# A graph network's messages: shares of target and features computed in input order and scattered as 2 KB rows, instead of small rows scattered and targets' rows gathered

## The chip, the cores and the metric

The kernel runs on one core of a Trainium2 chip. A core has TensorE (matrix products into PSUM), VectorE, ScalarE, GpSimd and SyncE, which run side by side and wait for each other through semaphores, and 16 DMA engines that move data between HBM and SBUF. DMAs are issued by SyncE and ScalarE (for transfers whose addresses are known to the issuing engine) and by GpSimd (for indirect ones, whose row numbers lie in SBUF). The metric is the device time of the whole program in microseconds, the median of several runs.

## The reference

3125 nodes have 256 features each; 50000 edges have a source, a target and 16 features. The edges come sorted by target; the sources are random, and the targets are dense at low numbers (3125 u², with u uniform). The computation, with `LN` a layer norm without weights:

```python
h = relu(LN(x))
msg = relu(concat(h[src], h[dst], edge_attr) @ mW1 + mb1)      # 50000 x 512
agg = segment_sum(msg @ mW2 + mb2, src)                        # by source
x = x + h + (relu(concat(h, agg) @ uW1 + ub1) @ uW2 + ub2)
g = relu(LN(x))
for W, b in three_layers:                                      # gelu between the layers
    g = D^-1/2 (A + I)^T D^-1/2 (g @ W) + b                    # A counts edges, D the in-degrees
out = x + g
```

The kernel splits `mW1` by rows: the source's share of a message is `h @ W1a`, the target's `h @ W1b`, the features' `edge_attr @ W1c`. The first two are tables with a row for each node (table A and table B). The sum by source comes ahead of `mW2`, which is linear.

## The kernel before, in words

**Names.** A node tile is 125 nodes; there are 25 of them (t). Node n belongs to tile n % 25. An edge tile is 128 edges of one source tile. "Products in two pieces" means that a fp32 value is split into a rounded part and a remainder (type fp32r), each multiplied in a pass of its own; plain fp32 products take two records each in the trace.

**Sort (L185 to L511).** The edges have to be grouped by source tile. They are dealt into 391 columns of 128; the first 240 columns are part 0, the last 151 part 1. For chunks of 24 columns `sort_chunk` (L330) makes each edge's place: keys are read back as broadcasts (L219), compared with the partition number (L336), counted by a running sum on VectorE (L345, L348), and turned by small products (L354). Each edge's payload is 20 numbers, 80 bytes: 16 features, target, source in its tile, column (L386 to L389). GpSimd scatters a column of 128 payloads by an indirect DMA (L170): part 0's columns in the sort, part 1's between the gathers of the next stage (L808). The places are first filled with an empty payload (L240, on ScalarE's queue). Two lists of work are laid between the chunks (L503 to L511): `tables` (L416: turns h, two fp32 products of 512 columns for each node tile at L427, and stores of table A, 4 KB a row in two pieces, L432, and table B, 2 KB a row, L437) and the counting of in-degrees (L456 to L486: one-hots on ScalarE at L470 and L473, comparisons on VectorE at L462).

**Messages (L588 to L826).** A flag in SBUF says whether the data keep the limits that the tiling assumes; it is read into a register and a branch chooses this path (L1067 to L1075). `order` (L776) runs over part 0, 25 targets' tiles of KT[0] = 11 edge tiles each, then part 1 with 7 each: 450 edge tiles. `load` (L620) fetches a tile's sorted payloads and 125 rows of table A. For each edge tile, `edge_tile` (L722) does:

```python
gather gb <- tabB[target]                       # GpSimd, L725, 128 rows of 2 KB
p  = payT @ wE                                  # features, L730
p += ohT @ apc                                  # source's share by a one-hot, two pieces, L732
gb += p                                         # VectorE, L733
m[0] = relu(gb); m[1] = max(gb, 0) - m[0]       # ScalarE L735, VectorE L736
p_sum += oh^T @ m                               # sum by source, two pieces, L746
```

One edge tile's sums are issued after the next one's `edge_tile`. Beside it goes `adjacency` of the step before (L704): counts of edges between nodes, as products of one-hots of sources and of targets (L681 on VectorE, 626 columns; L683 on TensorE, twice 313), for five ranges of targets, with 20 products of ranges in part 0 and 16 in part 1 for each tile. `counted` (L694) copies them to A as bytes; part 1 adds to what part 0 left (L701). Part 0's sums wait in HBM (`R_d`, L753) until part 1 fetches them (L759). In part 1, `node_steps` (L527) runs the node update of tile t - 2 beside (lines L539 to L574, TensorE tile `nd`).

**Graph layers and output (L951 to L1021).** 25 products with W (L974), then for 7 stretches of 448 columns 25 x 4 products with A (L1004), whose bytes VectorE and ScalarE turn into fp32r by turns (L998, L1000); three layers; then 25 transposed tiles are added to x and stored (L1021).

Of the kernel before, what the change touches and what calls it, by code (L numbers as in the profile page):

```python
# [19 lines left out]

# [10 lines left out]
BF16 = mybir.dt.bfloat16  # L31
# [10 lines left out]
NT, NP = 25, 125  # L42
EP, EC = 125, 400
SC = E // P
LEFT = E - P * SC
SCOLS = SC + 1
SPLIT = 240
CH = 24
CHUNKS = [(c, min(CH, e - c)) for b, e in ((0, SPLIT), (SPLIT, SCOLS)) for c in range(b, e, CH)]
PARTS = 2  # L50
KT = (11, 7)
NG, GT = 5, 5
GW = GT * NP
GS = GW + 1
HALF = GS // 2

REACH = (((0, 2), (1, 4), (3, 6), (5, 8), (6, 10)), ((0, 1), (0, 3), (1, 4), (3, 5), (4, 6)))
NB = NT * NG
AW = 448
NA = (NG * GS + AW - 1) // AW  # L60
NPAD = NA * AW
PW = 20
C_DST, C_PS, C_COL = ED, ED + 1, ED + 2
EPS = 1e-5
assert NT * NP == N and EP * EC == E and NB <= P and GS % 2 == 0


def col(c):

    return c // GT * GS + c % GT * NP  # L70
# [3 lines left out]
def gnn(ctx: ExitStack, tc: tile.TileContext, x, src, dst, ea, mW1, mb1, mW2, mb2, uW1, ub1, uW2,  # L74
# [3 lines left out]
    ORDER = mybir.DependencyInfo(mybir.DependencyClass.NoSync, mybir.DependencyReason.DATA)  # L78
# [5 lines left out]
    bk_d = dram.tile([SCOLS, P], BF16, name="bk_d")  # L84

    n_rows = [NT * k * P for k in KT]
    rows_d = [dram.tile([n + P * SCOLS, PW], F32, name=f"rows_d{q}") for q, n in enumerate(n_rows)]
    rows_v = [
        rows_d[q][:n_rows[q], :].rearrange("(t p k) w -> t p (k w)", p=P, k=KT[q])
        for q in range(PARTS)  # L90
    ]
    tabA = dram.tile([NT * NP, 2 * H], F32, name="tabA")
    tabB = dram.tile([N, H], F32, name="tabB")
    hT_d = dram.tile([NT, P, 2, NP], F32, name="hT_d")
    R_d = dram.tile([NT, NP, H], F32, name="R_d")
    xs_d = dram.tile([N, D], F32, name="xs_d")
    dis_d = dram.tile([NT, NP], F32, name="dis_d")
    xsv = xs_d.rearrange("(p c) f -> p c f", c=NT)
# [5 lines left out]
    key_s = g1.tile([P, SCOLS], I32, name="key_s")  # L104
    key_d = g1.tile([P, SCOLS], I32, name="key_d")
    for key, v in ((key_s, src), (key_d, dst)):
        nc.vector.memset(key[:, SC:], 0)
        nc.sync.dma_start(key[:, :SC], v[:P * SC].rearrange("(p c) -> p c", c=SC))
        nc.sync.dma_start(key[:LEFT, SC:], v[P * SC:].rearrange("(p o) -> p o", o=1))
# [4 lines left out]
    iota_i = g1.tile([P, P], I32, name="iota_i")  # L114
    nc.gpsimd.iota(iota_i, pattern=[[1, P]], base=0, channel_multiplier=0)
    iota_f = const.tile([P, P], F32, name="iota_f")
    nc.vector.tensor_copy(iota_f, iota_i)
    pid_i = g1.tile([P, 1], I32, name="pid_i")
# [4 lines left out]
    nc.vector.memset(ones, 1.0)  # L123

# [7 lines left out]
    dis = const.tile([NP, NT], F32, name="dis")  # L132
    flag = const.tile([1, 1], I32, name="flag")
    late = SCOLS - SPLIT
    pay1 = hold.tile([P, late, PW], F32, name="pay1")
    place1 = hold.tile([P, late], I32, name="place1")
# [12 lines left out]
    def ln_stats(pool, mv, row):  # L149
        st = pool.tile([NP, 6], F32, name="ln_st", bufs=3)  # L150
        nc.vector.bn_stats(st, row)
        nc.vector.bn_aggr(mv, st)

    def ln_scale(pool, mv):

        ve = pool.tile([NP, NT], F32, name="ln_ve")
        rstd = pool.tile([NP, NT], F32, name="ln_rstd")
        nmr = pool.tile([NP, NT], F32, name="ln_nmr")
        nc.vector.tensor_scalar(ve, mv[:, :, 1], EPS, None, op0=ALU.add)
        rsqrt(pool, rstd, ve, NP, NT)  # L160
        nc.vector.scalar_tensor_tensor(nmr, mv[:, :, 0], -1.0, rstd, op0=ALU.mult, op1=ALU.mult)
        return rstd, nmr


    fills = [[], []]
    scatters = [[], []]

    def scatter(q, place, pay, behind=None):

        s = nc.gpsimd.indirect_dma_start(  # L170
            out=rows_d[q], in_=pay, in_offset=None,
            out_offset=bass.IndirectOffsetOnAxis(ap=place, axis=0))
        tc.declare_no_dep(s.ins, group=f"rows{q}", reason="every edge has a place of its own")
        tc.add_to_no_dep_group(f"rows{q}", s.ins)
        for f in fills[q]:
            tc.add_manual_dep(s.ins, f.ins.name, SYNC, reason="places are filled first")
        if behind is not None:
            tc.add_manual_dep(s.ins, behind.ins.name, ORDER, reason="in turn with the gathers")
        scatters[q].append(s)

    def sorted_rows(q, load):
        for s in scatters[q]:
            tc.add_manual_dep(load.ins, s.ins.name, SYNC, reason="all rows are in place")

    with s1:  # L185
        gps = s1.enter_context(tc.tile_pool(name="gps", bufs=1, space=PSUM))
        ones_p = gps.tile([P, 1], F32, name="ones_p")
        nc.vector.memset(ones_p, 1.0)

        def parts_of(key, name):  # L190

            p_i = g1.tile([P, SCOLS], I32, name=f"p_{name}")
            c_f = g1.tile([P, SCOLS], F32, name=f"c_{name}")
            nc.vector.tensor_scalar(p_i, key, 5243.0, None, op0=ALU.mult)
            nc.vector.tensor_single_scalar(p_i, p_i, 17, op=ALU.logical_shift_right)
            nc.vector.scalar_tensor_tensor(c_f, p_i, -float(NT), key, op0=ALU.mult, op1=ALU.add)
            nc.vector.scalar_tensor_tensor(c_f[:, SC:], none, -64.0, c_f[:, SC:], op0=ALU.mult,
                                           op1=ALU.add)
            return p_i, c_f

        none = g1.tile([P, 1], F32, name="none")
        nc.vector.tensor_scalar(none, pid, LEFT - 0.5, None, op0=ALU.is_ge)
        psi, cs = parts_of(key_s, "s")
        pdi, cd = parts_of(key_d, "d")
        g_i = g1.tile([P, SCOLS], I32, name="g_i")
        nc.vector.tensor_scalar(g_i, cd, 13.0, None, op0=ALU.mult)
        nc.vector.tensor_single_scalar(g_i, g_i, 6, op=ALU.arith_shift_right)
        bkey = g1.tile([P, SCOLS], F32, name="bkey")
        nc.vector.scalar_tensor_tensor(bkey, cs, float(NG), g_i, op0=ALU.mult, op1=ALU.add)
        BT = P  # L210
        n_t = (SCOLS + BT - 1) // BT
        p_bk = gps.tile([P, n_t * P], F32, name="p_tab", bufs=2).rearrange("p (t a) -> p t a", a=P)
        bkT = g1.tile([P, n_t, P], BF16, name="bkT")
        bk = {}

        def load_keys(j):
            c0, w = CHUNKS[j]
            bk[j] = g1.tile([P, P * CH], BF16, name="bk", bufs=2)
            nc.sync.dma_start(  # L219
                bk[j][:, :P * w],  # L220
                bk_d[c0:c0 + w, :].rearrange("(o c) p -> o (c p)", o=1).to_broadcast([P, P * w]))

        for i in range(n_t):
            n = min(BT, SCOLS - i * BT)
            nc.tensor.transpose(p_bk[:n, i, :], bkey[:, i * BT:i * BT + n], ident)
        for i in range(n_t):
            n = min(BT, SCOLS - i * BT)
            nc.vector.tensor_copy(bkT[:n, i, :], p_bk[:n, i, :])
            nc.sync.dma_start(bk_d[i * BT:i * BT + n, :], bkT[:n, i, :])
            if i < 2:  # L230
                load_keys(i)


        fill = g1.tile([P, max(KT), PW], F32, name="fill")
        nc.gpsimd.memset(fill, 0.0)
        nc.gpsimd.memset(fill[:, :, C_PS:C_COL + 1], -1.0)
        for q in range(PARTS):
            for t in range(0, NT, GT):
                w = KT[q] * PW
                fills[q].append(nc.scalar.dma_start(  # L240
                    rows_v[q][t:t + GT].rearrange("t p w -> p t w"),
                    fill[:, :KT[q], :].rearrange("p k w -> p (k w)").unsqueeze(1)
                    .to_broadcast([P, GT, w])))


        cs_b = g1.tile([P, SCOLS], BF16, name="cs_b")
        nc.vector.tensor_copy(cs_b, cs)
        g_b = g1.tile([P, SCOLS], BF16, name="g_b")
        nc.vector.tensor_copy(g_b, g_i)
        eq_g = g1.tile([P, NG, SCOLS], BF16, name="eq_g")  # L250
        for b in range(NG):
            nc.vector.tensor_scalar(eq_g[:, b, :], g_b, float(b), None, op0=ALU.is_equal)
        eq_s = g1.tile([P, NT, SCOLS], BF16, name="eq_c", bufs=1)
        for b in range(NT):
            nc.vector.tensor_scalar(eq_s[:, b, :], cs_b, float(b), None, op0=ALU.is_equal)
        cnt = g1.tile([NT, PARTS, NG], F32, name="cnt")
# [73 lines left out]
        def sort_chunk(j):  # L330
# [6 lines left out]
            if j + 2 < len(CHUNKS):  # L337
                load_keys(j + 2)
# [100 lines left out]
        for c in range(NT):  # L439
            work.append(lambda c=c: tables(c))  # L440
# [661 lines left out]
```

## Time and profile before

| what | value |
|---|---|
| median of 3 runs | 2251.86 us (2247.84 to 2256.53) |
| the profiled execution | 2433.28 us, its span 2431.6 us |
| mean granted TensorE clock | 0.916 |
| TensorE busy | 1948.0 us, 80% of the span |
| VectorE busy | 1561.4 us, 64% |
| ScalarE busy | 1010.5 us, 42% |
| GpSimd busy | 858.9 us, 35% |
| moved by DMA | 242.64 MB, 100 GB/s over the span |
| chain that ended last | TensorE 58%, VectorE 12%, DMA 7%, ScalarE 5% |

The profiled execution is one run under the hardware profiler, and is longer than the runs that make the median; all rows of the profile belong to it. In a row of a group, `x450 | 454.6, 1010` means 450 instructions, 454.6 us busy in all, 1010 ns for one; what follows is the idle time of the engine just before them and what ended most of it. `PEld` is the loading of weights, which runs beside PE's products. In the list of queues the columns are packets, MB, and the time that the packets took as a share of the time of 16 DMA engines. "Issue" stands for time in which an engine waited for nothing that the profile shows.

### The profile page before, as it was taken

What the parts mean: (1) busy time and instruction counts of PE and PEld (TensorE: products, weight loads), DVE (VectorE), ACT (ScalarE), POOL (GpSimd) and SP (SyncE); (2) the same over time, 40 slices, a digit from 0 to 9 for tenths busy, and PEclk for the clock granted to TensorE, in tenths of its full rate; (3) what the DMA queues carried; (4) which work ended last, traced back from release to release, by engine and by line L of the source; (5) the groups of instructions that cost most, each with busy time, mean ns of one, the idle gap of its engine ahead of it and who ended that gap; (6) DMA issues with size and microseconds to landing.
All of it is one profiled execution on the core that took longest, in us unless ns stands there. A gap on an engine that the chain in (4) does not pass through costs nothing.

```text
span 2431.6 us, 30795 instructions
## 1 busy us (share of the span) xinstructions
PE 1948.0 (80%) x10314; PEld 1570.6 (65%) x10314; DVE 1561.4 (64%) x3618; ACT 1010.5 (42%) x2070; POOL 858.9 (35%) x895
## 2 busy tenths in 40 slices
PE   3224554675888888888889999999996999999993
PEld 3223232354665666665667888888885898998992
DVE  4636343595877888887879999999983323223221
ACT  0415443452444545454444444444433544434440
POOL 0656656304666666666653332333210000000000
PEclk9999666776999899999989999999997999999995
DMA  7102343325544444444444444444432000000003
GB/s 223 43 6 82 101 148 86 101 102 160 152 135 135 130 140 140 136 140 131 136 135 143 142 142 136 144 141 142 142 86 77 22 1 1 1 1 1 1 1 107
DMA packets 117792, 242.64 MB, mean 100 GB/s; under 512 B 19790, under 2 KB 65348, under 8 KB 117491
## 3 DMA queue, kind: packets, MB, share of 16 engines
q0 software_dynamic: 48512, 122.02, 18.5%
q1 hardware_dynamic: 55996, 103.64, 13.2%
q10 hardware_dynamic: 13108, 14.84, 2.0%
q8 instruction: 85, 1.39, 0.2%
q14 instruction: 91, 0.75, 0.1%
HBM read 193.31 MB, written 47.12 MB: 99 GB/s over the span
## 4 chain that ended last, share of the span: by engine, by line
PE 58%; DVE 12%; issue 7%; another core or an unknown queue 7%; DMA 7%; ACT 5%; POOL 2%; ACTq 1%; SPq 0%; DVEq 0%; POOLq 0%
PE p_o L1004 17%; PE p_A L683 8%; PE p_sum L746 7%; PE p_x L732 7%; PE nd L563 4%; PE p_x L730 3%; DVE gb L733 3%; PE p_g L974 2%; DVE od L681 2%; DVE m L736 2%; PE p_tab L427 2%; PE tr L665 2%; DMA out<-xrow 2%; PE nd L572 2%
## 5 line engine op out<-in xcount | busy, mean ns | idle before, releaser
L725 POOL DMA_INDIRECT gb<-tabB,rows x450 | 454.6, 1010 | 590.0 <-DVE m L736 410.2
L170 POOL DMA_INDIRECT rows_d<-pay,place x391 | 398.1, 1018 | 254.1 <-issue 116.6
L1004 PE MATMUL p_o<-a,g 125*128 125x448 f32 x2100 | 443.1, 370 | 0.0
L1004 PEld LDWEIGHTS p_o<-a,g 125*128 125x128 f32 x2100 | 394.7, 188 | 32.4 <-ACT g L976 0.3
L746 PE MATMUL p_sum<-m,oh 128*125 128x512 f32 x900 | 389.5, 466 | 18.8 <-issue 8.2
L735 ACT ACTIVATE m<-gb 128x512 fp32r<-128x512 f32 x450 | 283.4, 634 | 227.8 <-DVE gb L733 161.3
L683 PE MATMUL p_A<-od,oh_h 128*125 128x313 f16 x1800 | 360.5, 305 | 21.3 <-ACT A L697 11.1
L733 DVE TENSOR_TENSOR gb<-gb,p_x 128x512 f32<-128x512 f32 x450 | 305.0, 678 | 81.3 <-remote 24.7
L732 PE MATMUL p_x<-apc,ohT 125*128 125x512 f32 x900 | 344.5, 430 | 8.9 <-ACT ohT L667 6.7
L736 DVE SCALAR_TENSOR_TENSOR m<-gb,m 128x512 fp32r<-128x512 f32 x450 | 306.4, 684 | 64.7 <-ACT m L735 43.4
L681 DVE TENSOR_SCALAR od<-iota_h,dloc 128x626 f16<-128x626 f16 x900 | 331.6, 397 | 7.9 <-PE p_A L683 6.4
L683 PEld LDWEIGHTS <-oh_h 128*125 128x125 f16 x1800 | 246.8, 140 | 95.4 <-issue 35.0
L998 DVE CAST a<-A 125x448 fp32r<-125x448 uint8 x262 | 102.8, 393 | 273.7 <-PE p_o L1004 273.5
L1000 ACT CAST a<-A 125x448 fp32r<-125x448 uint8 x263 | 148.7, 566 | 240.8 <-PE p_o L1004 240.8
L730 PE MATMUL p_x<-wE,payT 128*128 128x512 f32 x450 | 209.7, 466 | 25.4 <-DVE gb L733 20.7
L746 PEld LDWEIGHTS p_sum<-m,oh 128*125 128x125 f32 x900 | 172.7, 196 | 80.5 <-ACT m L735 17.6
L732 PEld LDWEIGHTS p_x<-apc,ohT 125*128 125x128 f32 x900 | 174.7, 198 | 32.8 <-ACT ohT L667 13.3
L427 PE MATMUL p_tab<-wAB,hT 128*125 128x512 f32 x200 | 126.7, 791 | 73.6 <-issue 46.2
L354 PE MATMUL p_pos<-ones_r,q 128*128 128x2 f32 x391 | 83.0, 323 | 72.4 <-DVE carry L351 40.4
L427 PEld LDWEIGHTS p_tab<-wAB,hT 128*125 128x125 f32 x200 | 48.6, 256 | 134.5 <-issue 104.7
L354 PEld LDWEIGHTS p_pos<-ones_r,q 128*128 128x128 f32 x391 | 72.8, 262 | 86.8 <-issue 42.4
L668 ACT CAST oh_h<-oh 128x375 f16<-128x375 f32 (+1 forms) x125 | 71.2, 569 | 135.8 <-DVE oh L659 121.6
(193 smaller groups left out, 2437.9 us busy)
## 6 DMA issues: line engine op xcount, KB each, us to landing
apc<-tabA SPq DMA_DIRECT2D x50, 500.0 KB
tabA<-a_sb SPq DMA_DIRECT2D x25, 500.0 KB
bk<-bk_d SPq DMA_DIRECT2D x16, 768.0 KB
gb<-tabB,rows POOLq DMA_INDIRECT x450
rows_d<-pay,place POOLq DMA_INDIRECT x391
tabB<-b_sb SPq DMA_DIRECT2D x25, 250.0 KB
R_d<-R SPq DMA_DIRECT2D x25, 250.0 KB
R<-R_d SPq DMA_DIRECT2D x25, 250.0 KB
```

Of the source, the lines that this page charges most:

```text
L170: s = nc.gpsimd.indirect_dma_start(out=rows_d[q], in_=pay, in_offset=None, out_offset=bass.IndirectOffsetOnAxis(ap=place, axis=0))
L427: nc.tensor.matmul(p, hT[:, k, :], wAB[:, s, k, :], start=k == 0, stop=k == 1)
L681: nc.vector.tensor_scalar(od, iota_h, dloc[q, t][:, g, k:k + 1], None, op0=ALU.is_equal)
L683: nc.tensor.matmul(p[:, h_, :HALF], oh_h[q, t][:, k, :], od[:, h_ * HALF:(h_ + 1) * HALF], start=k == lo, stop=k == hi)
L725: gathers[0] = nc.gpsimd.indirect_dma_start(out=gb, out_offset=None, in_=tabB, in_offset=bass.IndirectOffsetOnAxis(ap=row[q, t][:, k, C_DS ...
L730: nc.tensor.matmul(p, payT[q, t][:, k // 2, :], wE[k % 2], start=True, stop=False)
L732: nc.tensor.matmul(p, ohT, apc[q, t][:, s, :], start=False, stop=s == 1)
L733: nc.vector.tensor_add(gb, gb, p)
L735: nc.scalar.activation(m[:, 0, :], gb, AF.Relu)
L736: nc.vector.scalar_tensor_tensor(m[:, 1, :], gb, 0.0, m[:, 0, :].bitcast(F32), op0=ALU.max, op1=ALU.subtract)
L746: nc.tensor.matmul(p_sum[t], oh, m[:, s, :], start=k == 0 and s == 0, stop=k == KT[q] - 1 and s == 1)
L1004: nc.tensor.matmul(po[:, f, :AW], g[:, s, q, f * P:(f + 1) * P], a, start=s == 0 and q == 0, stop=s == NT - 1 and q == 1)
```

## The change

Node n now belongs to tile n // 125 (L240, a product and a shift). The 391 columns of edges become 66 blocks of 768 consecutive edges, which, being sorted by target, have targets in a stretch of 128 nodes. The places come from products with a triangular matrix for all edges at once (L269 to L291). The stage has three pieces.

*The lead (to L443).* Keys and x are loaded; ScalarE issues a fill of zeros, 20.3 MB in runs of 6.3 KB, after x has landed (L216); LN, relu and transposes of h; GpSimd adds h and ub2 to x for the residual (L402, L403, 50 additions of 256 columns); table B in two pieces, 4 KB a row (26 products of 512 columns, each of two fp32 halves; 13 stores of 1 MB).

*The blocks of z (L446 to L593).* For each block a register is loaded with the first target of its stretch, and 128 rows of table B are loaded from there; features are split in two pieces and transposed; targets' one-hots come from a broadcast product. TensorE forms the features' plus the target's share, 512 numbers for each edge, ScalarE and VectorE copy them from PSUM, and GpSimd scatters them with the source's and target's number as rows of 2112 bytes, 391 scatters in all. Beside this go table A's products and stores (13 of 1 MB, on ScalarE's queue) and the counting of sources.

*Messages.* One pass over 25 tiles of 17 edge tiles: 425. Rows are loaded in groups of 4, 4, 3, 3 and 3 edge tiles into three buffers. The one-hots of targets are 14131 columns wide for each tile t in all. The in-degrees are read from A when all counts are there (L829 to L856). The node update runs for t - 1, with one buffer for each of its tiles.

```diff
-KT = (11, 7)
+BLK = MB * P
+KT = 17
+ZW = 528
...
+        fill = nc.scalar.dma_start(
+            rows_d[:ROWS, :].rearrange("(t s) w -> t s w", s=CAP)[:, SURE:, :]
+            .rearrange("t (p i) w -> p t (i w)", p=P),
+            zero.unsqueeze(1).to_broadcast([P, NT, (KT - SURE // P) * ZW]))
+        for v in x_in:
+            tc.add_manual_dep(fill.ins, v.ins.name, SYNC, reason="x is wanted first")
...
+        def window(b):
+            bw[b] = z1.tile([P, 2 * H], F32R, name="bw", bufs=4)
+            eng = nc.scalar if b % 3 == 2 else nc.sync
+            reg = eng.value_load(w0_i[0:1, b:b + 1], min_val=0, max_val=N - P)
+            eng.dma_start(bw[b].bitcast(F32), tabB[bass.ds(reg, P), :])
...
+        def block(b):
+            z = zt[b % 3]
+            cols = range(MB) if b < NB - 1 else (MB - 1,)
+            nc.vector.tensor_copy(z[:, :, H:H + 2], ends[:, :, b, :])
+            for j0 in range(0, MB, 2):
...
+                p = gps.tile([P, 2, H], F32, name="p_z", bufs=2)
+                for j in js:
+                    o = p[:, j - j0, :]
+                    nc.tensor.matmul(o, pay[b][:, j // 2, :], wE[j % 2], start=True, stop=False)
+                    for s in range(2):
+                        nc.tensor.matmul(o, one[b][:, j, :], bw[b][:, s * H:(s + 1) * H],
+                                         start=False, stop=s == 1)
+                a, e = js[0], js[-1] + 1
+                (nc.vector.tensor_copy if j0 == 2 else nc.scalar.copy)(
+                    z[:, a:e, :H], p[:, a - j0:e - j0, :])
+                for j in js:
+                    s = nc.gpsimd.indirect_dma_start(
+                        out=rows_d, in_=z[:, j, :], in_offset=None,
+                        out_offset=bass.IndirectOffsetOnAxis(ap=place[:, j, b:b + 1], axis=0))
...
+        def store_A(c):
+            def f(b, e, n, v):
+                nc.scalar.dma_start(tabAv[c + b:c + e, :NP, :].rearrange("t p f -> p t f"), v)
+            return f
...
+        def load_rows(t, i):
+            a, e = GROUPS[i]
+            v = mp.tile([P, 4, ZW], F32, name="z", bufs=3)[:, :e - a, :]
+            o = nc.sync.dma_start(
+                v, rows_d[t * CAP + a * P:t * CAP + e * P, :].rearrange("(k p) w -> p k w", p=P))
+            for s in scatters:
+                tc.add_manual_dep(o.ins, s.ins.name, SYNC, reason="all rows are in place")
...
-        def edge_tile(q, t, k):
-            oh, ohT = onehot[q, t, k]
-            gb = mp.tile([P, H], F32, name="gb", bufs=5)
-            gathers[0] = nc.gpsimd.indirect_dma_start(
-                out=gb, out_offset=None, in_=tabB,
-                in_offset=bass.IndirectOffsetOnAxis(
-                    ap=row[q, t][:, k, C_DST:C_DST + 1].bitcast(I32), axis=0))
+        def edge_tile(t, k):
+            oh, ohT, zr = onehot[t, k]
             p = mps.tile([P, H], F32, name="p_x", bufs=2)
-            nc.tensor.matmul(p, payT[q, t][:, k // 2, :], wE[k % 2], start=True, stop=False)
             for s in range(2):
-                nc.tensor.matmul(p, ohT, apc[q, t][:, s, :], start=False, stop=s == 1)
-            nc.vector.tensor_add(gb, gb, p)
+                nc.tensor.matmul(p, ohT, apc[t][:, s, :], start=s == 0, stop=s == 1)
+            gb = mp.tile([P, H], F32, name="gb", bufs=3)
+            nc.vector.tensor_add(gb, zr, p)
```

## The prediction

> **What bounds the kernel now.** I read the split by stage first, because the busy shares of the page mix stages with different limits. The stage borders come from the trace: the flag that opens the messages is read at about 557 us, part 0 ends at 1294, the messages at 1847, and the first large graph product starts at 1905.
>
> ```profile
> core 0: us, PE busy (x) PEld busy (x) DVE busy (x) ACT busy (x) POOL busy (x), PEclk, DMA share, GB/s
> 0.00:60.00 60.00, 23.87 (x407) 22.83 (x407) 25.58 (x108) 4.39 (x16) 3.48 (x44) 1.00 0.73 222
> 60.00:557.00 497.00, 234.17 (x1025) 154.26 (x1025) 268.01 (x567) 205.17 (x547) 241.52 (x250) 0.80 0.29 84
> 557.00:1294.00 737.00, 620.51 (x2890) 452.41 (x2891) 583.15 (x1253) 354.03 (x640) 458.55 (x437) 0.91 0.49 141
> 1294.00:1847.00 553.00, 544.99 (x3494) 477.13 (x3493) 510.52 (x1301) 220.54 (x436) 155.31 (x164) 0.99 0.44 129
> ...
> 1905.00:2375.00 470.00, 468.86 (x2291) 426.33 (x2289) 147.42 (x333) 193.34 (x352) 0.00 (x0) 1.00 0.01 1
> ```
>
> In the sort (60 to 557) no engine is busy for more than 54% of the time; it is a chain that changes engine. Part 1 (553 us) and the graph layers (470 us) are TensorE's, with VectorE at 92% in part 1. Part 0 (737 us) has TensorE at 84% and GpSimd at 62%. The granted clock in the messages is 0.91 and 0.99, so the clock is not the limit there.
>
> The chain of waits shows TensorE's own period in part 1: the same step of the node update ends on the chain every 21.82 us.
>
> ```profile
> 1.71 30.07 DMA xt<-in_x
> ...
> 1354.28 1.78 PE nd L563 x16
> ...
> 1376.10 1.78 PE nd L563 x16
> ```
>
> From such rows come prices back to back: 1.78/16 = 0.111 us for a fp32 pass of 125 columns, 0.203 us for 448 columns (117.57 us for 580 products of the graph layers), so 0.232 for 512 and 0.142 for 313. One target of part 1 is then 7 tiles x 5 x 0.232 = 8.1, 11 transposes = 1.2, 32 count products x 0.142 = 4.5, node update 7.95 (48 passes of 0.111, 8 of 0.216, ten-odd short ones): 21.8 us. The model gives the period exactly, and I use it for the changed loop.
>
> The costly groups give what GpSimd pays for an indirect transfer, and the list of queues what such bytes cost:
>
> ```profile
> L725 POOL DMA_INDIRECT gb<-tabB,rows x450 | 454.6, 1010 | 590.0 <-DVE m L736 410.2
> L170 POOL DMA_INDIRECT rows_d<-pay,place x391 | 398.1, 1018 | 254.1 <-issue 116.6
> ```
>
> ```profile
> q0 software_dynamic: 48512, 122.02, 18.5%
> ```
>
> A scatter takes 1.02 us of GpSimd, with 0.30 us after it in which it waits for nothing visible. Queue q0 held 0.185 x 16 x 2431.6 = 7197 engine-us for 122 MB, nearly all gathered rows: 59 ns per KB on an engine. Scatters of 80-byte rows alone are seen from 150 to 200 us, in the list of queues of that stretch:
>
> ```profile
> q0 software_dynamic: 768, 0.25, 3.1%
> ```
>
> That is 0.031 x 16 x 50 = 24.8 engine-us for 0.25 MB, 99 ns per KB, in packets of some 325 bytes.
>
> **The new message loop.** Gathers (450), their rows, the payload products of 512 columns (450), the transposes of payloads, R's way through HBM, the second pass over A (L701) and the second part's waste (450 tiles become 425) leave. There remain, for each of 25 targets' tiles, 17 edge tiles with two p_x and two sum products each: 68 x 0.232 = 15.8 us; 17 transposes 1.9; counts over ranges of 14131 columns in all (part 0 and 1 had 36 x 626 = 22536) x 0.203/448 = 6.4; node update 7.95. TensorE: 32.0 us. VectorE by part 1's durations: gb 17 x 0.68 = 11.5, m 11.6, one-hots 3.0, small ones 1.5, targets 14131/626 x 0.39 = 8.9, node 1.3: 37.8. Part 1's durations sum to 24.8 for each target against 20.4 us busy (510.5/25), a factor 0.825 for overlapping ends: 31.2 us. Two engines stand within 3% of each other, so I take 34 us a period (bounds 32.5, TensorE alone with part 1's fill of 98.5%, and 37, where they take turns). ScalarE has 17 x 0.63 + 7 copies, some 20 us, and hides. Row loads are 4.6 MB in a period, 135 GB/s, what part 0 already carried at 0.49 of the queues; three buffers of four tiles cover them. Sum: 14 us of hand-over and first rows, 24 for the first target, 24 x 34 = 816, 40 at the end (31 before, and 10 for the in-degrees that now come last): 894, where the two parts took 737 + 553 = 1290. Gain 396 us.
>
> **The lead to the first scatter.** ScalarE issues x's loads, then the 20 MB fill. Before, issuing 6400 small runs kept it until 53.9 us; now 3200 runs of 6.3 KB follow x's landing at about 32 us: free at 41 if issue alone counts, at 125 if the whole fill must land (20.3 MB at 222 GB/s); I take 55, as the queue takes part of them. Ranks by products cost TensorE and VectorE little, beside x. Then 66 register loads of window starts, 22 on ScalarE ahead of its own relus: the only row near is the hand-over, where flag, register, branch and first DMA take 4 us (88 us for 22); the page "DMA: Bandwidth & Descriptors" of the Trainium skill (Latency and other measured facts) has a floor of about 0.6 us (13 us). I take 25. Fifty GpSimd additions of 256 columns (0.3 to 0.7 us, the lower from VectorE's 0.68 for 512) trail by up to 35 us, 26 products of table B and their stores 57 us (L427: 1.27 us a product). First scatter: about 170 us (bounds 125 to 230).
>
> **The z blocks.** 66 blocks, each with six scatters of 128 rows of 2112 B. GpSimd: 391 x (1.02 + 0.30) = 516 us. Queues, for one block: six scatters of 264 KB x 59 ns/KB / 16 = 5.98 us, a window of 512 KB 1.6 us, features 0.15: 7.75, x 66 = 512 us. TensorE has 5.4 us a block, ScalarE and VectorE about 4 each. Two equal limits of 512 us that rarely coincide, so some is added. No row shows scatters of 2 KB rows: by size they are like the gathers (59 ns/KB), by direction like the small scatters (99). I take 59, because 2 KB rows were the gathers' size too and small packets cost more for each byte; 99 is the upper bound, and a rival. Two rules bear on the sum.
>
> First, VectorE beside descriptor writing. The timeline of the sort has
>
> ```profile
> 134.14 0.96 POOL L170 DMA_INDIRECT rows_d<-pay,place  x1 [0.30 <-issue]
> 135.25 0.27 DVE L462 TENSOR_SCALAR eq_c<-cs_b 128x391 bf16<-128x391 bf16 x1 [1.13 <-issue]
> 135.40 0.96 POOL L170 DMA_INDIRECT rows_d<-pay,place  x1 [0.30 <-issue]
> 136.65 0.32 DVE L462 TENSOR_SCALAR eq_c<-cs_b 128x391 bf16<-128x391 bf16 x1 [1.14 <-issue]
> ```
>
> VectorE, with 0.27 us of work in each and nothing to wait for, gets one through for each scatter, 1.26 us apart. The Trainium skill's "SBUF — State Buffer", Who interferes with whom, says why: both engines share a port pair under an exclusive lock, and an operation in a two-port mode waits for the whole of the other's. VectorE's 3 or 4 such operations of a block would wait 1.1 us each: 4 + 4.3 = 8.3 us, 548 us in all. Had the operations other forms, 4 us a block would hide and z would stay at 512.
>
> Second, table A's stores (13 of 1 MB, in the first 20 blocks). x's load above is 3.2 MB on 125 partitions and took 30.07 us: 106 GB/s while all queues moved 222. The skill's "DMA: Bandwidth & Descriptors" (Why a DMA increments its semaphore by 16 and not by 1) gives a transfer the largest number of engines up to 16 that divides its slowest dimension: 125 partitions get 5. By it 12.8 MB at 49.5 ns/KB (queue q1) are 127 us on each of five engines instead of 40 on all: those engines, which also carry scatters, end up to 85 us late. Without the rule z would be 512; with both I take 595 (bounds 430, where GpSimd's 0.30 vanishes and the queues run ahead, and 660).
>
> **Sum.** 170 + 595 + 894 + 585 for the graph layers and output, which keep their sizes, = 2244 us of span against 2431.6. The profiled execution took 2433.28 us, 181 more than the median of 2251.86, and the trace doesn't say where. Spread evenly, the new median is 2251.86 x 2244/2431.6 = 2078. If all of it lies in sort and part 0 (1294 us, which then are 1113 outside the profile), the lead and z shrink by the same 0.86 and the others not: 658 + 894 + 585 = 2137. I take 2105.
>
> **Rivals.**
> - *Likeliest* (0.50): as summed, 2040 to 2160.
> - *Cheap scatters* (0.18): GpSimd issues every 1.0 us and the stores hide; z is about 440, 155 us less, some 1965 (1930 to 2040). For it: 1.018 is the mean in the sort, and part of the 0.30 may be the wait for places. Against: 381 of its 391 waits are named issue.
> - *TensorE and VectorE alternate in the loop* (0.19): 37 us a period, +75: 2180 (2160 to 2240). For it: part 0, with both at 79 to 84%, never filled either. Against: part 1.
> - *Slower than before* (0.10): writing rows to HBM costs more than reading them. From the median, 147 us more in z eat the gain: z of 742; without the 83 us that I added for stores and ports, 659, or 10.0 us a block; less 1.75 for window and features, 8.2 us for 48 rows on each engine: 172 ns a row, 83 ns/KB. Above that it is slower; with the small scatters' 99 ns/KB a block takes 6 x 264 x 99/16 = 9.8, + 1.75 = 11.55 us, z 11.55 x 66 + 83 = 845, and the time is 2105 + 250 x 0.93 (2105/2244, to the median's scale) = 2340 (2263 to 2400). For it: the small scatters themselves. Against: their packets are a sixth of these rows.
> - *No change* (0.03): two of the bad ends together, 2240 to 2263.
>
> A measurement of this kernel can tell about 0.5% from no change, 11 us. Faster 0.87, same 0.03, slower 0.10. The range leaves out the slow case, no change and the low end of cheap scatters: 1975 to 2220.
>
> **What would show it.** In the changed profile: scatters about 1.3 us apart and z near 9 us a block; GpSimd's idle time named as its own issue, not a DMA; on five queues more time than on the others in the first 20 blocks; the node update's step every 34 us with TensorE and VectorE both over 90%; first scatter near 170 us; graph layers at 470. I am wrong if scatters wait for earlier scatters through z's buffers (rows dearer than the 122 ns of 59 ns/KB), or if loop periods pass 37.

## The result: no change, and the profile after

The changed kernel takes 2257.95 us (median of 16 runs) beside 2256.35 us of the kernel before (16 runs): a ratio of 1.0006, interval 0.9993 to 1.002. The forecast was 2105, with a range of 1975 to 2220. Its profiled execution has a span of 2256.6 us, 12.6 us from the 2244 that the prediction summed. So the sum for the new kernel held to 0.6%, and the baseline that it was scaled by did not. The table of stretches of the changed kernel (span, then busy time of each engine, granted clock, share of the DMA engines, GB/s):

```profile
core 0: us, PE busy (x) PEld busy (x) DVE busy (x) ACT busy (x) POOL busy (x), PEclk, DMA share, GB/s
0.00:60.00 60.00, 9.62 (x59) 6.81 (x59) 32.84 (x127) 7.70 (x14) 10.72 (x38) 1.00 0.95 356
60.00:180.00 120.00, 84.77 (x253) 40.69 (x253) 84.46 (x165) 30.95 (x47) 32.34 (x49) 0.80 0.59 221
180.00:800.00 620.00, 455.35 (x1947) 329.53 (x1945) 258.75 (x458) 168.93 (x208) 384.65 (x391) 0.85 0.71 247
...
860.00:1652.00 792.00, 790.85 (x4479) 626.66 (x4478) 741.86 (x1648) 493.34 (x965) 0.00 (x0) 1.00 0.50 161
...
1731.00:2199.00 468.00, 467.90 (x2287) 425.55 (x2286) 145.75 (x330) 192.98 (x351) 0.00 (x0) 1.00 0.00 1
```

The lead ends at 180, the z blocks run to about 800, the message loop has TensorE busy for 99.9% of its time, and the graph layers take 468 us, as before. Below stand two of the costliest groups of the changed kernel, its scatters and the addition that took the old gathers' rows, and then five of its waits in the z blocks (total, times, longest):

```profile
L537 POOL DMA_INDIRECT rows_d<-zt,place x391 | 384.7, 984 | 250.0 <-ACT zt L534 101.8
L758 DVE TENSOR_TENSOR gb<-z,p_x 128x512 f32<-128x512 f32 x425 | 289.5, 682 | 22.6 <-PE p_x L756 19.6
```

```profile
DVE zt L521 <- DMA rows_d<-zt,place: 228.7, 58, 13.1
POOL rows_d L537 <- ACT zt L534: 101.8, 29, 25.4
POOL rows_d L537 <- issue: 91.4, 300, 0.3
...
ACT a_sb L417 <- DMA tabA<-a_sb: 52.1, 8, 10.1
...
DVE zt L534 <- issue: 0.4, 2, 0.2
```

GpSimd pays 0.98 us for a scatter in the mean and 0.3 us behind it, near the 1.02 and 0.30 of the forecast; ScalarE waits for table A's stores eight times. VectorE stands 228.7 us for z's buffers, whose rows are still being scattered.

### The profile page after: what moved, and what is told of

It is laid out like the page before. It is cut to its first block, busy times and chain, and to the rows that moved or that the text cites. A ratio compares the mean times of both kernels' runs of the same rounds, so it can differ in the third digit from the quotient of the medians.

```text
span 2256.6 us, 27379 instructions
## 1 busy us (share of the span) xinstructions
PE 1922.6 (85%) x9541; PEld 1509.0 (67%) x9541; DVE 1341.7 (59%) x2903; ACT 961.9 (43%) x1728; POOL 427.7 (19%) x477
## 5 line engine op out<-in xcount | busy, mean ns | idle before, releaser
L537 POOL DMA_INDIRECT rows_d<-zt,place x391 | 384.7, 984 | 250.0 <-ACT zt L534 101.8
L756 PE MATMUL p_x<-apc,ohT 126*128 126x512 f32 x850 | 325.0, 452 | 1.0 <-ACT ohT L712 0.9
L758 DVE TENSOR_TENSOR gb<-z,p_x 128x512 f32<-128x512 f32 x425 | 289.5, 682 | 22.6 <-PE p_x L756 19.6
L531 PE MATMUL p_z<-bw,ohd 128*128 128x512 f32 x782 | 287.6, 453 | 0.0
L534 ACT COPY zt<-p_z 128x1024 f32<-128x1024 f32 x131 | 132.3, 1010 | 300.6 <-PE p_z L531 288.1
L529 PE MATMUL p_z<-wE,payT 128*128 128x512 f32 x391 | 185.0, 473 | 75.7 <-DVE zt L534 51.4
L729 PE MATMUL p_A<-od,oh_h 128*126 128x448 f16 (+2 forms) x1000 | 230.0, 315 | 0.3 <-DVE od L722 0.3
L531 PEld LDWEIGHTS p_z<-bw,ohd 128*128 128x128 f32 x782 | 171.2, 221 | 52.1 <-issue 19.6
L722 DVE TENSOR_SCALAR od<-iota_h,dloc 128x896 f16<-128x896 f16 (+16 forms) x425 | 176.3, 433 | 0.5 <-PE p_A L729 0.2
L756 PEld LDWEIGHTS p_x<-apc,ohT 126*128 126x128 f32 x850 | 150.9, 191 | 22.0 <-ACT ohT L712 2.2
L521 DVE COPY zt<-ends 128x12 f32<-128x12 f32 x66 | 13.1, 198 | 228.8 <-DMA rows_d<-zt,place 228.7
```

Of the source, the lines that this page charges most:

```text
L529: nc.tensor.matmul(o, pay[b][:, j // 2, :], wE[j % 2], start=True, stop=False)
L531: nc.tensor.matmul(o, one[b][:, j, :], bw[b][:, s * H:(s + 1) * H], start=False, stop=s == 1)
L537: s = nc.gpsimd.indirect_dma_start(out=rows_d, in_=z[:, j, :], in_offset=None, out_offset=bass.IndirectOffsetOnAxis(ap=place[:, j, b:b + 1 ...
L722: nc.vector.tensor_scalar(targets[k][:, :WIDTH[k]], iota_h[:, :WIDTH[k]], dloc[t][:, k:k + 1], None, op0=ALU.is_equal)
L729: nc.tensor.matmul(p_A[g][:, l - g * AW:h - g * AW], oh_h[t][:, k, :], targets[k][:, l - FIRST[k]:h - FIRST[k]], start=start, stop=stop)
L756: nc.tensor.matmul(p, ohT, apc[t][:, s, :], start=s == 0, stop=s == 1)
```

## The experiments

Runs were taken in sets: the kernels of one set ran side by side with the kernel before, and each ratio below is to the kernel before in the same set.

**First: which baseline?** Theory: the 175 us by which the first profile exceeded the runs of the kernel before belong to that execution. Rival: profiling slows the kernel before. Three more kernels cut it (and the changed one) into stages.

e1, the kernel before unchanged. 

> The kernel before, unchanged, profiled a second time. Theory (the 175 us by which its first profiled execution exceeded its runs belong to that one execution, not to the kernel): a new span of 2250 to 2265 us, like the runs, and by stage sort + part 0 shorter by about 175 us. Rival (profiling itself slows something that the kernel before has and the changed one has not): a span of about 2430 again beside runs of 2256.

e2, the kernel before up to the end of the sort (the loop over the two branches is replaced):

```diff
-    for f, fast, general in ((flag, messages, messages_by_column), (flag2, gcn, gcn_by_column)):
...
+    nc.sync.dma_start(out, xs_d)
```

> The kernel before up to the end of the sort; messages and graph layers are left out and the residual is copied to the output. In the first profile the sort took 557 us. If the 175 us lie in the sort: about 385 + 25 for the copy. If they lie in part 0 of the messages: about 557 + 25. If evenly spread: about 515 + 25.

e3, the same copy behind the messages. 

> The kernel before without the graph layers; the output is a copy of the node features after the messages. In the first profile this point was at 1847 us. If all of the 175 us lie ahead of it: about 1672 + 25. If evenly spread: 1710 + 25. Less the time of the sort alone it gives the messages' own time.

e4, the changed kernel up to the end of the z blocks, with the same copy. 

> The changed kernel up to the end of the z blocks; messages and graph layers are left out and the residual is copied to the output. Its profile has this point at about 810 us. Whatever the theory, 810 + 25; against the sort alone it gives what the new stage costs more: about 425 us if the sort really takes 385, 250 if it takes 557.

Measured: e1 2267.44 us (ratio 1.0005, 0.9965 to 1.0046), its profile's span 2265.4. e2 489.58, e3 1699.34, e4 816.8. e1's profiled execution lies among its other runs (2260.7 to 2271.2), so the profiler is not the cause; the first profile showed a longer execution. e3 fits the case of all the excess ahead of the layers (1672 + 25); e2 fits none of its three (410, 582 and 540). Stretches of e1:

```profile
core 0: us, PE busy (x) PEld busy (x) DVE busy (x) ACT busy (x) POOL busy (x), PEclk, DMA share, GB/s
...
60.00:490.00 430.00, 225.51 (x1025) 150.32 (x1025) 264.40 (x565) 203.23 (x547) 243.95 (x250) 0.82 0.33 97
490.00:1130.00 640.00, 588.50 (x2906) 428.43 (x2907) 584.91 (x1259) 354.03 (x644) 464.85 (x438) 0.98 0.56 163
1130.00:1679.00 549.00, 541.56 (x3473) 474.09 (x3472) 507.33 (x1293) 218.25 (x432) 154.40 (x163) 0.99 0.44 129
```

The sort takes 490 us instead of 557 and part 0 640 instead of 737; part 1 and the layers are the same. By two marks: the first p_x product comes at 507.4 instead of 574.0 (67 us earlier), and from there to the first graph product (p_g) it is 1188.0 instead of 1287.6 (100 less). Together 166 us, the whole difference of the spans. The shares of the chain that ended last hint at what it was. The kernel before, first profile (the table at the top of this document lists four of these):

```profile
PE 58%; DVE 12%; issue 7%; another core or an unknown queue 7%; DMA 7%; ACT 5%; POOL 2%; ACTq 1%; SPq 0%; DVEq 0%; POOLq 0%
```

and of e1:

```profile
PE 50%; DVE 17%; DMA 17%; POOL 8%; issue 7%; ACT 2%; DVEq 0%; SPq 0%; ACTq 0%; POOLq 0%
```

"Another core or an unknown queue" was 7.4% of 2431.6 us, 180 us, on a kernel that runs on one core. In e1 the entry is gone. Its size is that of the excess, but its parts are not: of the pieces that the chain lists, 110 us are in the sort and 68 in part 0, where the marks give 67 and 100. In part 0 TensorE was also busy for longer, 620.5 us against 588.5, at a granted clock of 0.91 against 0.98 (the stretches in the prediction and above). What such a wait looks like, in the first profile's timeline, where it is named "remote":

```profile
787.78 0.96 POOL L725 DMA_INDIRECT gb<-tabB,rows  x1 [0.30 <-issue]
...
790.50 0.69 DVE L733 TENSOR_TENSOR gb<-gb,p_x 128x512 f32<-128x512 f32 x1 [3.38 <-remote]
790.59 0.58 ACT L653 CAST payT<-tr 128x512 fp32r<-128x512 f32 x1 [6.75 <-remote]
```

ScalarE stands although what it needs is recorded as made (TensorE's transposes ended by 786.8), and VectorE and ScalarE go on within 0.1 us of each other.

**Second: why do the z blocks take 620 us, not 512?** Theory: ScalarE, in order, waits for the store of table A's last piece with the blocks' copies behind it. Rivals: the five engines of a 125-partition store (the prediction's second rule); VectorE and GpSimd holding each other up (its first); the queues as a whole.

e5 lays table A's 13 pieces evenly over the 66 blocks:

```diff
-        while tests:
-            work.append(tests.pop(0))
+        n_a, n_t = len(work), len(tests)
+        for i in range(n_a, 0, -1):
+            while len(tests) > n_t * (i - 1) // n_a:
+                work.insert(i, tests.pop())
```

> The changed kernel with table A's 13 pieces laid evenly over the 66 blocks instead of one after the other at their start. Theory (the z stage has a slow first half because each piece's copy on ScalarE waits for the store of the piece ahead of it, 25 us on five engines, with the blocks' own copies queued behind; after that GpSimd sets 6 x 1.26 = 7.6 us a block): z from 640 to about 520 us, the kernel about 120 us faster, 2140. Rival (queues are the limit, the same bytes remain): z stays at about 620, within 1% of 2257.

e6 issues each store as two:

```diff
-                nc.scalar.dma_start(tabAv[c + b:c + e, :NP, :].rearrange("t p f -> p t f"), v)
+                for p0, p1 in ((0, 112), (112, NP)):
+                    nc.scalar.dma_start(
+                        tabAv[c + b:c + e, p0:p1, :].rearrange("t p f -> p t f"), v[p0:p1])
```

> The changed kernel with each of table A's stores issued as two, of 112 and of 13 partitions. If stores are slow because 125 partitions are spread over five engines, 112 partitions take 16 of them and a store lands in some 10 us instead of 25: waits for it vanish and z falls by 60 to 110 us, 2150 to 2200. If they are slow because all queues are full of scatters: no change, 2257.

e7 has both. 

> Both edits. If each of them alone removes the wait, together no more than the better one: about 2140. If GpSimd's 1.26 us for each of 391 scatters are the floor, z cannot be under 493 us, so the kernel not under about 2115.

e8 has e5's edit, and the middle copy on ScalarE:

```diff
-                (nc.vector.tensor_copy if j0 == 2 else nc.scalar.copy)(
+                nc.scalar.copy(
```

> The even spread, and the middle copy out of PSUM on ScalarE too, so that VectorE has one long operation less in each block. If VectorE and GpSimd hold each other up in z (the exclusive port pair), this gains up to 1.2 us a block, 80 us, on the spread alone; if GpSimd's own rate is the floor: no difference to the spread alone (within 0.5%), or a loss where ScalarE's three copies of 1.0 us come late.

Measured: 2283.17, 2273.98, 2281.08, 2276.62 us; but in this set the kernel before took 2430.17 us (7 runs, 2424.9 to 2443.1). Ratios 0.940 (0.935 to 0.946), 0.935 (0.931 to 0.939), 0.936 (0.931 to 0.940) and 0.935 (0.931 to 0.939). The waits named "remote" are back in every one of the four profiles, all of them in the z blocks. So the first profile was no accident of one execution (though the three runs beside it took 2248 to 2257 us): whole sets of runs have these waits, and others don't. The four runs can't tell z's rivals apart, since every form of z came out within 0.4%, with these waits in it.

**Third: the same again, beside the changed kernel.** e9 is the changed kernel. 

> The changed kernel, unchanged, beside the kernel before on one chip. The kernel before has now taken 2265 us on one chip and 2430 us on another, with waits that no row explains on the second. Theory (the chip makes the difference, and the changed kernel pays less for it): where the kernel before takes about 2430, the changed one takes 2260 to 2285, a ratio of 0.935; where it takes about 2260, the ratio is 1.00. Rival (the changed kernel pays the same 165 us on such a chip): 2425 there.

e10 is e5's kernel. 

> Table A's 13 pieces laid evenly over the 66 blocks, now beside the changed kernel itself. On a chip without the unexplained waits: z about 520 us instead of 640, some 2140, if the store waits were the cause of the slow first half; equal to the changed kernel if the queues are. On the chip with them it took 2283, and equal to the changed kernel is then expected.

e11 is e6's kernel. 

> Table A's stores split into 112 and 13 partitions, beside the changed kernel. By five engines for 125 partitions: a store lands in some 10 us instead of 25, ScalarE's waits for it go, 60 to 110 us less on a chip without unexplained waits. By full queues: no change.

e12 leaves out 150 of part 0's late scatters in the kernel before:

```diff
-                    while late_done < want:
+                    while late_done < min(want, 1):
```

> The kernel before with one of the 151 late scatters of part 0; the other 150, and so part 1's rows, are left out (part 1 works on the filler rows at the same cost). If the unexplained waits come with scatters in flight: on a chip where the kernel before takes 2430, part 0 falls from 720 to about 630 us and shows none, 2340 in all; on one where it takes 2256, under 15 us are gained, since TensorE is at 94% in part 0. If they come with the chip alone: no change on either.

The kernel before took 2262.41 us, and none of the four profiles has a "remote" wait. This set and the one before are both recorded on chip 0, with the kernel before at 2262 and at 2430; if the number names one chip, the chip alone does not make the difference. e9 2261.18 (ratio 1.0005, 0.9989 to 1.0021). e10 2263.73 (1.0001, 0.9985 to 1.0017): its ScalarE no longer waits for a store of table A at all (52.1 us in the changed kernel), and z takes as long (617.7 us from the first to the last scatter), so the theory of ScalarE's wait falls. Its scatters are slowed evenly instead, 64 to 73 in each 100 us from 300 to 800. e11 2220.4 (0.982, 0.979 to 0.985): 41 us less than e9. e12 2227.61 (0.986, 0.982 to 0.989): 35 us less than the kernel before, more than the 15 expected.

e13 is e7's kernel. 

> Split stores and even spread together. Split stores alone gave 2220 (ratio 0.982), the spread alone nothing (1.000). If the stores cost z only through the five engines that carry them, their place in z does not matter and both together equal the split alone, 2215 to 2225. If a wait of ScalarE for a store is left that the spread removes: 2180 to 2200.

e14 stores the first of table A's pieces alone, and the messages read tiles 0 and 1 of the table for all:

```diff
+                if c == 0:
                     nc.scalar.dma_start(tabAv[c + b:c + e, :NP, :].rearrange("t p f -> p t f"), v)
...
-            nc.sync.dma_start(apc[t].rearrange("p s f -> p (s f)").bitcast(F32), tabAv[t])
+            nc.sync.dma_start(apc[t].rearrange("p s f -> p (s f)").bitcast(F32), tabAv[t % 2])
```

> The changed kernel with the first of table A's 13 stores alone (12 MB less written; the messages then read the first two tiles of the table for every tile, at the same cost). It prices the stores as a whole. By the five engines (127 us on each against 40 on all): 85 us as forecast, of which the split gave back 41; so z about 555 and the kernel about 2175. If the split gave back all that the stores cost: 2220. If stores cost z all of its excess over GpSimd's 500 us: 2120.

Another set with the kernel before at 2434.19: e13 2275.66, e14 2275.14 (both 0.935 to 0.936), again with "remote" waits in z. Their z takes 632 and 629 us from the first to the last scatter, with the stores and without twelve of them, so this set can't price the stores.

e15 (the changed kernel), e16 (e7's), e17 (e14's) and e18 (e12's) once more. 

> The changed kernel beside the kernel before, a third time. In sets of runs in which the kernel before takes 2430, no run of the changed one itself is there yet. Such a set: 2270 to 2285 if it pays like its variants (2274 to 2283), 2425 if it pays like the kernel before. A set with the kernel before at 2260: 2260 again.

> Split stores and even spread together. In a set with the kernel before at 2260: 2215 to 2225 (place does not matter) or 2180 to 2200 (a wait is left that the spread removes). In a set with the kernel before at 2430: 2275 as before.

> One of table A's 13 stores (the messages read the first two tiles of the table for every tile). In a set with the kernel before at 2260: 2175 if all stores cost the 85 us forecast, 2220 if the split gave back all that they cost, 2120 if they are the whole excess of z. In a set with the kernel before at 2430: 2275 as before, since there every form of z took the same time.

> The kernel before with one of its 151 late scatters (part 1 works on the filler rows). In a set with the kernel before at 2260 it gained 35 us. In one with the kernel before at 2430: 2340 or less, and no unexplained waits in part 0, if those come with scatters in flight; 2395 if they come from something else.

The kernel before took 2266.84 us. e15 2263.49 (0.998, 0.996 to 1.000), e16 2246.8 (0.992, 0.990 to 0.995), e17 2209.95 (0.975, 0.970 to 0.979), e18 2233.56 (0.984, 0.979 to 0.989). The twelve stores that e17 leaves out cost 53 us (2263 to 2210), of the 85 forecast, and the split gave back 41. Spread and split together gain 17 us, less than the split alone and less than either expectation of e16: once the stores are split, spreading them loses time (2247 us against e11's 2220, in two sets), and why is open. e18 is again 33 us below the kernel before. In stretches of 100 us, the changed kernel:

```profile
300.00:400.00 100.00, 79.92 (x366) 56.52 (x366) 50.70 (x77) 23.25 (x29) 48.79 (x46) 0.83 0.65 219
...
600.00:700.00 100.00, 75.69 (x313) 55.31 (x311) 38.17 (x78) 32.21 (x41) 75.91 (x80) 0.91 0.83 287
```

e11:

```profile
300.00:400.00 100.00, 82.34 (x371) 53.62 (x369) 51.41 (x87) 30.05 (x37) 61.64 (x60) 0.98 0.85 288
...
600.00:700.00 100.00, 79.32 (x312) 58.06 (x311) 38.82 (x79) 32.41 (x40) 75.93 (x80) 0.87 0.81 284
```

and e17, early:

```profile
300.00:400.00 100.00, 90.30 (x424) 60.78 (x423) 57.74 (x92) 31.74 (x39) 63.38 (x63) 0.94 0.65 226
```

Late in z the first two both issue 80 scatters in 100 us: 75.9 us busy and 80 x 0.30 = 24 behind them, so GpSimd is full, 7.6 us a block. Early, while table A is made, the changed kernel issues 46 and e11 60; e11 moves 288 GB/s there instead of 219, and its granted clock is 0.98 instead of 0.83. e17 issues no more than 63, with TensorE busy for 90% of the time: between 200 and 400 us it also forms table A (L412, 52.1 us by the products' own durations) and counts sources (L550, 33.8 us). That points to TensorE as the next limit there; it is read from the trace, and no run tests it.

## Why the prediction was wrong

- *The step that failed* is the baseline: "181 more than the median of 2251.86, and the trace doesn't say where. Spread evenly ...". The excess was in the profiled execution of the kernel before and not in the runs that make its median, and the trace did hint at it: the chain has an entry of that size, 180 us, released by nothing that the profile shows. e1, without such waits, has a span of 2265 us, and the sum of 2244 for the new kernel is within 1% of it: no change. Both of the prediction's ways of scaling gave the new kernel a share of an excess that its runs did not have. The gain of 396 us in the messages was taken from 1290, which held 100 us of it; marks of e1 and the changed kernel give 1188.0 to 869.4, a gain of 319. The first message was to come 779 - 574 = 205 us later; it comes at 821.0 instead of 507.4, 314 later. 319 against 314: what the messages gained was given back ahead of the loop.
- *The ratio in the longer sets* fits, by luck. In sets in which the kernel before takes 2430 to 2434, forms of the changed kernel take 2274 to 2283, 0.935 to 0.940; the forecast was 2105/2252 = 0.935. But 2105 was a choice between two ways of scaling an excess whose place was not known, and "remote" waits in z were no part of it. The same forms take 19 to 65 us more in these sets than in the others, where the kernel before takes 167 more. The changed kernel itself was not measured in such a set.
- *Loop*: 34 us a period forecast; R's copies (L775) run from 851.9 to 1655.9, 33.5 us. TensorE is busy for 99.9% and VectorE for 94% of the loop, and the rival of 37 us is out. From the last scatter to the layers it is 881 us, of 894.
- *Lead*: 170 forecast, first scatter at 180.6. A part was off: the fill was issued at 19.0 us, in 0.4 us, where the prediction held ScalarE until 55. No profile here times the 66 register loads one by one, so the floor that the prediction cites for them stays unchecked.
- *z*: 595 forecast, 618 from the first to the end of the last scatter, inside its bounds, but with other parts, so the nearness is in part luck. Waits for z's buffers, which the prediction named as a sign of being wrong, did come (VectorE's 228.7 us), but with cheap rows. The queue of scatters held 45.1% of 16 x 620 us for 105.5 MB, 42 ns/KB and not 59, so the queues were no second limit late in z, where GpSimd is full, and the rival on the far side (83 ns/KB) is out. (The prediction's 5.98 us a block counts six scatters as 270 KB each, its 9.8 as 264; this 2% changes nothing.) The row of that queue from 180 to 800 us:

```profile
q0 software_dynamic: 31210, 105.50, 45.1%
```

- *Stores and ports*, 83 us together: the stores are 53 of it. That 112 and 13 partitions cost less than 125 agrees with the page "DMA: Bandwidth & Descriptors" of the Trainium skill (section Why a DMA increments its semaphore by 16 and not by 1), which gives a transfer the largest number of engines up to 16 that divides its slowest dimension, 16 for 112 and 5 for 125; no profile here shows the engines one by one, and a split into two of other sizes was not tried. VectorE's stalls behind descriptor writing, 36 us of the 83, don't show: in the sort they stood as waits named issue of 1.13 us, and in z such waits of VectorE sum to 0.4 us. (e8 against e5 was to test this; they differ by 0.3%, in a set with "remote" waits.) Of z's 618 us, 391 x 1.26 = 493 are GpSimd's and 53 the stores'; the remaining 72 lie in its first 270 us, beside the making of table A, where e17 points to TensorE.
- *Layers and output*: 585 forecast, 577 (from about 1680 to 2257).

The split stores (e11, 2220 us) beat both kernels, by 1.8%.

## What to carry to other kernels

If a profiled execution is longer than the runs, find the excess before using any total from it. A share of the chain with no known releaser, on one core and of the size of the excess, is the first suspect; profiling the unchanged kernel once more settled it here. A forecast must compare both kernels with the excess or both without it. When work is moved from a loop into a stage of its own, price the new stage against GpSimd's time for each indirect transfer (here 1.26 us, 493 us in all) before counting the loop's gain. A store laid on 125 partitions may be worth splitting into 112 and 13 (here 41 us for 13 stores beside scatters).

## What the runs showed of the hardware that was not expected

The same kernel took 2256 to 2267 us in four sets of runs and 2430 to 2434 in two. In the profiles of the long kind, waits named "remote" stand in the sort and part 0 of the kernel before (289 and 106 us summed over engines) or in the z blocks (151 to 249 in e5 to e8, e13 and e14), the stages with indirect scatters to HBM, and none in part 1, which has gathers alone, nor in the layers. That they follow the scatters is read from this, and not shown: the run that leaves scatters out (e12, e18) fell both times in sets without such waits. What causes them, and why some sets have them, stays open; both kinds are recorded on chip 0.
